# Layer 2 of a four-layer block: one combined weight for attention's way out and the context

## The chip, the cores and the metric

The kernel runs on one NeuronCore of a Trainium2 chip. Five engines work side by side, each through its own list of instructions in order: TensorE (PE in the profile, with its weight loads as PEld), VectorE (DVE), ScalarE (ACT), GpSimd (POOL) and SyncE (SP, which issues most of the DMA). They wait for each other by semaphores. The metric is the device time of one execution in microseconds (us); smaller is better. Two kernels are compared by executions on the same chip.

## What is computed

The program is four layers over x of shape 8 x 512 x 128 (float32). Each layer has a sequence mixer s and a gate g, and adds s times silu(g) to x. The change lies in the mixer of layer 2, which after a layernorm and causal attention with 16 heads does this (cut to what matters):

```python
attn = attn @ out_w + out_b
x = x + attn
ctx = attn.reshape(b * s, d)
xs = _ln(x, g1, b1).reshape(b * s, d)
vs = jnp.zeros_like(xs)
def step(carry, _):
    xs, vs = carry
    u = jnp.tanh(ctx @ w_ctx + xs @ w_x + b_inl)
    vn = vs + DT * (u - xs - vs)
    xn_ = xs + DT * vn
    return ((xn_, vn), None)
(xs, vs), _ = jax.lax.scan(step, (xs, vs), None, length=NUM_ITERS)   # 8
x = x + xs.reshape(b, s, d)
h = _ln(x, g2, b2)
x = x + (gelu(h @ ff_w1 + ff_b1) @ ff_w2 + ff_b2)
```

`attn` is used twice: added to x, and, through `w_ctx`, as a constant term of the eight steps of the recurrence. The gate of layer 2 is a feed-forward net of five products with two gelu layers of width 512 (`ffn` in the kernel).

## The kernel before

**Layout.** A sequence has 512 tokens. Tiles are either token-major (128 tokens on the partitions, 4 tiles of 128 features) or feature-major (128 features on the partitions, 512 tokens along the row). Matmuls give feature-major results from a weight as the stationary operand; a change of layout is four PE transposes (`to_features`, L168) and a copy out of PSUM.

**Units.** `layer2` walks over 128 units: 8 sequences, 4 head groups g, 4 key blocks kc. Per unit PE is given, in this order: the scores of the unit in `weights` (L1462, output `pu<-qT,kT`, which ACT turns into exp at L1498); a first `fill`; the scores for the row maxima of a unit nine ahead in `maxima` (L1462, output `pu<-kT,qT`, with the causal mask added at L1474 and the maximum taken by DVE at L1477 into `mpad`); a second `fill`; and the weighted sums of the unit two behind in `sums` (L1511). Widths go with kc: scores of 512, 384, 256 and 128 columns, and maxima of 512 columns (a 128x1024 reduction for two heads) once in four units. `put_maxima` (L1484, L1488) subtracts the maxima for a pair of groups.

**Fills.** Everything else comes as generators whose steps are put between these. `fill` takes one step of `groups` if there is one, otherwise one step of `rest` (but none in the second fill of an even unit), and then as many steps of `front` as a credit in passes allows. The number that a step yields is its charge.

- `front` is `begin` of the next sequence (layernorm, transposes to `xT2` and, with scale and bias on DVE at L172, `xa2`; projections L1395 and L1398 to `kT2` and `qT2`, L1409 to `va2`), and its `ffn` (L1427/L1428, then L1443 with gelu at L1444, then L1451).
- `groups` is `group`: for each head group, L1525 to `yb2`. After the last group of a sequence it goes on with `yb2` transposed to `yT2` (a step), the product with `out_w` in both layouts (L1539, added to `xn2` on DVE at L1540; and L1542, evacuated by ACT as `ctx2` at L1544; a step), and the product with `w_ctx` (L1547, copied by ACT to `cw2` at L1549; a step).
- `rest` follows when `group` is at its end: the layernorm of `xn2` into `hr2` (one step; L1286, L1288, L1304 on ACT, L1306, L1310, L1296 on POOL, L1290), its transposes L168 (a step), eight iterations (L1565 on PE, L1567 on DVE, tanh L1568 on ACT, L1572 and L1573 on DVE; each a step), the transposes L1578 with L1579 on DVE and the second layernorm into `hr2` (one step), L168 and L172 (a step), L1588 with gelu at L1589 (two steps of two products), and L1596 (two steps).

The steps of sequence b's `group` end and `rest` thus run among the units of sequence b+1. What is left after the last unit, the end of `group` and the `rest` of sequence 7, is handed to layer 3 as `k.tail`, which takes one step of it per unit of its own.

**Order.** On PE the order of the program text is kept (`manual_schedule`). In layer 2 a scheduler sets the order on DVE, ACT and POOL. PSUM banks are given out by tag: two for `pa` (all products above but the scores, sums and L1443), two pairs for `pu`, one each for `pf` and `ph`. A product waits until the last reader of its bank's former content is through.

Of the kernel before, what the change touches and what calls it, by code (L numbers as in the profile page):

```python
# [10 lines left out]
F32 = mybir.dt.float32  # L11
# [3 lines left out]
AF = mybir.ActivationFunctionType  # L15
# [5 lines left out]
P = 128  # L21
B = 8
T = 512
# [12 lines left out]
class Pack:  # L36


    def __init__(self):
        self.parts, self.at, self.n = [], {}, 0  # L40
# [32 lines left out]
def bc(ap, axis, n):  # L73

    a = ap.unsqueeze(axis)
    shape = list(a.shape)
    shape[axis] = n
    return a.to_broadcast(shape)
# [889 lines left out]
class Layer1:  # L968
# [40 lines left out]
    @staticmethod  # L1009
    def by_head(va):  # L1010
        return va[:, :, 0 : H * 9].rearrange("p j (h d) -> p j h d", d=9)
# [302 lines left out]
class Layer2(BySequence):  # L1314


    def __init__(self, k, ctx, late, x, A, at):
        self.k, self.x = k, x
        nc, tc = k.nc, k.tc

        pool = lambda name, bufs=1: ctx.enter_context(
            tc.tile_pool(name="l2" + name, bufs=bufs, reuse_waits="tile", side="left")
        )
        right = lambda name, bufs=1: late.enter_context(
            tc.tile_pool(name="l2" + name, bufs=bufs, reuse_waits="tile", side="right")
        )
        cp = right("c")
        self.cn = cn = k.load_consts(cp, A["c2"], at[0], "c2")
        ap = pool("f")
        self.fn = fn = k.load_consts(ap, A["f2"], at[1], "f2")  # L1330

        self.half_s = ap.tile([P, 4], F32, name="half_s")
        nc.vector.tensor_scalar(self.half_s, fn["w1_s"], 0.5, None, ALU.mult)
        self.both_s = ap.tile([P, 4], F32, name="both_s")
        nc.vector.tensor_tensor(self.both_s, self.half_s, fn["w2_s"], ALU.mult)
        self.out_bc = cp.tile([P, 1], F32, name="out_bc")
        nc.vector.tensor_scalar(self.out_bc, cn["out_bc"], 100.0, None, ALU.mult)


        self.g1 = cp.tile([P, 2], F32, name="g1_2")  # L1340
        nc.vector.tensor_scalar(self.g1[:, 0:1], cn["g1"], 100.0, None, ALU.mult)
        nc.vector.tensor_scalar(self.g1[:, 1:2], cn["b1"], 100.0, None, ALU.mult)

        self.va2 = [ap.tile([P, JT, H * 9 + 23], F32, name=f"va2{i}") for i in range(2)]
        for t in self.va2:
            nc.gpsimd.memset(t, 0.0)
            nc.gpsimd.memset(self.by_head(t)[:, :, :, 8:9], 1.0)

        self.mpad = [ap.tile([P, JT, P], F32, name=f"mpad{i}") for i in range(2)]
        for t in self.mpad:  # L1350
            nc.gpsimd.memset(t, 0.0)
        self.sp2 = right("p", 2)
        self.tp = right("t", 2)
        self.bp = pool("b", 2)
        self.ep = pool("e", LAG + 2)
        self.q = {}

    @staticmethod
    def by_head(va):
        return va[:, :, 0 : H * 9].rearrange("p j (h d) -> p j h d", d=9)  # L1360

    def begin(self, b):

# [155 lines left out]
    def group(self, b, g):  # L1519

        k, nc, cn, tp, q = self.k, self.k.nc, self.cn, self.tp, self.q[b]
        oT = q["oT"]
        ps = k.pa((P, JT, P))
        for qt in range(JT):
            nc.tensor.transpose(ps[:, qt, :], oT[:, qt * P : (qt + 1) * P], k.ident)  # L1525
        v = ps.rearrange("p t (h d) -> p t h d", d=32)
        den = self.sp2.tile([P, JT, 4], F32, name="den2")
        nc.vector.reciprocal(den, v[:, :, :, 8])
        o = q["yb"].rearrange("p t (a i v d) -> p t a i v d", a=2, i=4, v=2)[:, :, g // 2, :, g % 2, :]
        nc.vector.tensor_tensor(o, v[:, :, :, 0:8], bc(den, 3, 8), ALU.mult)  # L1530
        yield 1.25
        if g < 3:
            return
        sT = tp.tile([P, T], F32, name="yT2", bufs=1)
        k.to_features(q["yb"], sT, nt=JT)
        yield 1.25
        ps = k.pa((P, JT, C))
        for j in range(JT):
            nc.tensor.matmul(ps[:, j, :], sT[:, j * P : (j + 1) * P], cn["out_w"], start=True, stop=True)  # L1539
        nc.vector.tensor_tensor(q["xn"], q["xn"], ps, ALU.add)  # L1540
        ps = k.pa()
        nc.tensor.matmul(ps, cn["out_w"], sT, start=True, stop=True)  # L1542
        ctx = tp.tile([P, T], F32, name="ctx2", bufs=1)
        nc.scalar.activation(ctx, ps, AF.Identity, bias=self.out_bc, scale=100.0)  # L1544
        yield 2.25
        ps = k.pa()
        nc.tensor.matmul(ps, cn["w_ctx"], ctx, start=True, stop=True)  # L1547
        q["ctx"] = tp.tile([P, T], F32, name="cw2")
        nc.scalar.copy(q["ctx"], ps)  # L1549
        yield 1.0  # L1550

    def rest(self, b):

# [61 lines left out]
def layer2(k, x, A, at):  # L1615

    late = ExitStack()
    with ExitStack() as ctx:
        ctx.enter_context(k.banks("l2p", pu=2, pf=1, pa=2, ph=1))
        L = Layer2(k, ctx, late, x, A, at)  # L1620
        units = [(b, g, kc) for b in range(B) for g in range(4) for kc in range(JT)]
        held = {}
        ctx.enter_context(k.tc.manual_schedule(engines={mybir.EngineType.PE}))
        for _ in L.begin(0):
            pass
        U = 4 * JT
        PAIR = 2 * JT
        AHEAD = PAIR + 1
        def maxima(u):

            b, g, n = units[u]
            L.maxima(b, g, (n - 1) % JT)

        first = L.ffn(0)
        for u in range(AHEAD):
            maxima(u)
            next(first, None)
        L.put_maxima(0, 0)
        for _ in first:
            pass  # L1640
        front = groups = rest = iter(())
        credit = 0.0

        def fill(u, second):


            nonlocal credit
            wide = 1.5 - u % JT
            share = (2.4 + 0.6 * wide, 2.4 - 0.6 * wide)[second] if u >= U else 1.8
            share += 0.3 - 0.6 * second  # L1650
            passes = next(groups, None)
            if passes is None:
                passes = 0.0 if second and u % 2 == 0 else next(rest, 0.0)
            credit = min(credit, share) + share - passes
            while credit > 0.0:
                passes = next(front, None)
                if passes is None:
                    break
                credit -= passes

        for u in range(len(units) + LAG):
            b, n = divmod(u, U)
            if u < len(units):
                held[u] = L.weights(*units[u])
                if u % PAIR == PAIR - 1 and u + 1 < len(units):
                    L.put_maxima(units[u + 1][0], units[u + 1][1] // 2)
            fill(u, False)
            if u + AHEAD < len(units):
                maxima(u + AHEAD)
            fill(u, True)  # L1670
            if u >= LAG:
                wb, g, kc = units[u - LAG]
                L.sums(wb, g, kc, held.pop(u - LAG))
                if kc == JT - 1:
                    groups = chain(groups, L.group(wb, g))
                    if g == 3:
                        rest = chain(rest, L.rest(wb))

            if n == LAG - 1 and b + 1 < B:
                front = chain(L.begin(b + 1), front, L.ffn(b + 1))  # L1680
        assert next(front, None) is None
        k.tail = chain(groups, rest), late.close
# [634 lines left out]

PACKS = (pack0, pack1, pack2, pack3)
LAYERS = (layer0, layer1, layer2, layer3)


# [35 lines left out]
```

## Time and profile before

The time before is 3589.2 us, the median of three runs (3583.16 to 3598.02). One execution was profiled.

| | us |
|---|---|
| profiled execution, whole | 3592.12 |
| its span, first to last instruction | 3590.4 |
| layer 2's units in it, from 1461 to 2560 | 1099 |
| PE / DVE / ACT / POOL busy, whole span | 2891.0 / 2323.1 / 1793.6 / 733.4 |
| mean granted TensorE clock, whole span | 0.861 |
| ACT table loads at L1498, L1444, L1589 | 66, 55, 14 of 1.283 us |

How to read it: a matmul in float32 appears as two PE rows, so L1547's eight products are "x16". "Idle before" of a group is time in which its engine had nothing running just before an instruction of the group, with the releaser that ended it. PEld is a queue of its own in the profile: a wait there need not hold up PE if a matmul is still running. PEclk is the granted share of TensorE's full clock. In timeline rows the columns are start, duration, engine, line, operation, names and shape, count, and in brackets the idle time before with its releaser. The notation `128x512` is partitions by elements.

### The profile page before, as it was taken

To read this page: it belongs to the slowest core of one execution; us is meant where nothing else is said; L and a number is where in the kernel's file an instruction comes from. 1 tells how busy PE (TensorE), PEld (TensorE's weight loads), DVE (VectorE), ACT (ScalarE), POOL (GpSimd) and SP (SyncE) were. 2 spreads that over 40 slices of the span, in tenths; PEclk is the share of its full clock that TensorE was granted. 3 is DMA by queue.
4 is the path that set the end of the run, shared out by engine and by line. 5 is a ranking of instruction groups with operands and counts; after the bars stand their busy time and mean duration, and the time that the engine had idled before them with its cause. 6 is when DMAs were issued, how large, how long until landed. Compare 5 with 4: busy or idle time off the path is not lost.

```text
span 3590.4 us, 46304 instructions
## 1 busy us (share of the span) xinstructions
PE 2891.0 (81%) x16950; PEld 1591.5 (44%) x16950; DVE 2323.1 (65%) x6354; ACT 1793.6 (50%) x3386; POOL 733.4 (20%) x845
## 2 busy tenths in 40 slices
PE   6175868635998799698888888898789888888887
PEld 4154656534444454334434333443334444454453
DVE  7999888896583334534454554554577767777776
ACT  4173646422444355243545454455466556566655
POOL 0012131300124553211111111111112122222221
PEclk8587889766789999898999999999788888888888
DMA  4012121211001222100000000000000000000000
GB/s 121 2 30 44 32 52 32 43 49 48 1 13 35 40 42 27 45 1 1 1 1 1 1 1 1 1 1 1 21 1 1 4 1 4 4 1 7 4 1 6
DMA packets 67522, 64.59 MB, mean 18 GB/s; under 512 B 5344, under 2 KB 59616, under 8 KB 66784
## 3 DMA queue, kind: packets, MB, share of 16 engines
q1 hardware_dynamic: 39264, 42.75, 3.9%
q0 software_dynamic: 19712, 14.69, 3.1%
q10 hardware_dynamic: 8320, 4.19, 0.4%
q8 instruction: 133, 2.18, 0.2%
q14 instruction: 93, 0.76, 0.1%
HBM read 43.80 MB, written 17.83 MB: 17 GB/s over the span
## 4 chain that ended last, share of the span: by engine, by line
PE 36%; DVE 14%; ACT 10%; issue 2%; POOL 1%; DMA 0%; POOLq 0%; ACTq 0%; DVEq 0%
PE pu L1462 6%; PE ph L1443 5%; PE pu L2102 4%; DVE nm L2104 3%; PE pf L2132 2%; ACT at L2107 2%; PE pf L1511 2%; ACT at L1498 2%; ACT L1498 2%; DVE mpad L1477 1%; PE pa L1565 1%; PE pa L2145 1%; PE pu L1474 1%; PE pa L1596 1%; PE pa L2034 1%
## 5 line engine op out<-in xcount | busy, mean ns | idle before, releaser
L2107 ACT ACTIVATE at<-pu,nm 128x512 f32<-128x512 f32 x512 | 347.7, 690 | 226.8 <-DVE nm L2104 225.3
L2102 PE MATMUL pu<-qT,kT 32*128 32x512 f32 x1024 | 296.3, 740 | 79.3 <-ACT at L2107 79.1
L2104 DVE TENSOR_REDUCE nm<-pu 128x1 f32<-128x512 f32 x512 | 318.7, 680 | 39.6 <-PE pu L2102 39.2
L199 POOL TENSOR_SCALAR_AFFINE_SELECT at<-at 128x512 f32<-128x512 f32 x184 | 124.4, 676 | 1029.2 <-ACT at L1498 879.7
L1477 DVE TENSOR_REDUCE mpad<-pu 128x2 f32<-128x1024 f32 (+3 forms) x256 | 198.9, 818 | 151.1 <-PE pu L1474 151.0
L1128 ACT ACTIVATE at<-pu,rsqrt 128x1024 f32<-128x1024 f32 (+3 forms) x256 | 190.9, 792 | 188.2 <-PE pu L1123 164.1
L1443 PE MATMUL ph<-hid,f 128*128 128x512 f32 x512 | 256.9, 629 | 11.6 <-ACT hid L1444 11.5
L1498 ACT ACTIVATE at<-pu 128x1024 f32<-128x1024 f32 (+3 forms) x256 | 167.1, 701 | 163.6 <-PE pu L1462 162.5
L364 PE MATMUL pa<-HR,ident 128*128 128x128 f32 x512 | 127.4, 417 | 140.3 <-DVE HR L765 140.3
L2102 PEld LDWEIGHTS pu<-qT,kT 32*128 32x128 f32 x1024 | 100.2, 209 | 178.4 <-ACT at L2107 159.4
L364 PEld LDWEIGHTS pa<-HR,ident 128*128 128x128 f32 x512 | 112.4, 265 | 150.1 <-DVE HR L765 74.7
L2132 PE MATMUL pf<-at,va 128*32 128x512 f32 x1024 | 161.3, 708 | 11.9 <-POOL va L2119 11.9
L608 POOL DMA_INDIRECT f_d<-ys,idx x48 | 90.3, 1881 | 382.2 <-ACT ys L607 352.8
L1462 PE MATMUL pu<-kT,qT 32*128 32x512 f32 (+3 forms) x1024 | 136.2, 504 | 30.4 <-ACT at L1498 29.6
L1443 PEld LDWEIGHTS ph<-hid,f 128*128 128x128 f32 x512 | 94.8, 200 | 114.1 <-issue 90.1
L1462 PE MATMUL pu<-qT,kT 32*128 32x512 f32 (+3 forms) x1024 | 128.1, 496 | 20.3 <-DVE mpad L1477 19.9
L1123 PE MATMUL pu<-qT,kT 32*128 32x512 f32 (+3 forms) x1024 | 131.4, 519 | 5.8 <-ACT at L1128 4.9
L2119 POOL TENSOR_TENSOR va<-V,sm 128x32 f32<-128x32 f32 x128 | 34.5, 270 | 488.8 <-DVE sm L2118 428.6
L1066 POOL DMA_INDIRECT f_d<-ys,idx x64 | 103.4, 1616 | 135.1 <-DMA f_d<-ys,idx 86.1
L1498 ACT ACT_TABLE_LOAD x66 | 84.7, 1283 | 90.1 <-PE pu L1462 89.3
L1133 DVE TENSOR_TENSOR at<-at,ceiling 128x512 f32<-128x512 f32 x72 | 49.9, 694 | 106.5 <-ACT at L1128 102.5
L691 ACT COPY Y<-pa 128x128 f32<-128x128 f32 x32 | 8.4, 263 | 208.4 <-PE pa L364 208.4
(621 smaller groups left out, 6806.2 us busy)
## 6 DMA issues: line engine op xcount, KB each, us to landing
w<-in_w_dram SPq DMA_DIRECT2D x24, 512.0 KB
f_d<-zeros ACTq DMA_DIRECT2D x8, 512.0 KB, 5.7
xn_d<-xn SPq DMA_DIRECT2D x8, 512.0 KB, 3.2
w<-in_w_dram SPq DMA_DIRECT2D x16, 256.0 KB, 2.9
w<-in_w_dram SPq DMA_DIRECT2D x24, 128.0 KB, 2.1
f<-in_f_dram SPq DMA_DIRECT2D x1, 2888.0 KB
xn<-in_x_dram SPq DMA_DIRECT2D x4, 512.0 KB, 7.1
Gt<-in_x_dram SPq DMA_DIRECT2D x4, 512.0 KB, 5.0
```

The lines of the kernel that those rows point to most:

```text
L199: self.nc.gpsimd.affine_select(a, a if src is None else src, pattern, ALU.is_ge, 0.0, base=0, channel_multiplier=-1)
L364: nc.tensor.matmul(ps, k.ident, src[:, :, i], start=(i == 0), stop=(i == 7))
L1123: nc.tensor.matmul(pu[:, n, 0:m], q["kT"][r, g // 2, kc * P : kc * P + P], q["qT"][r, g, kc * P :], start=True, stop=True,)
L1128: nc.scalar.activation(at_[:, i : i + 2, 0:m], pu[:, :, 0:m], AF.Square, bias=k.rsqrt2, scale=32.0**-0.5)
L1443: nc.tensor.matmul(ps, fn[n][:, c0 : c0 + P], src[:, i, :], start=(i == 0), stop=(i == 3))
L1462: self.k.nc.tensor.matmul(pu[:, n, 0:m], a[r, c0 : c0 + P], b[r, q0 : q0 + m], start=True, stop=stop)
L1477: nc.vector.tensor_reduce(top[:, i : i + 2, 16 + g % 2], pu[:, :, 0:m], AX.X, ALU.max)
L1498: nc.scalar.activation(at_[:, i : i + 2, 0:m], pu[:, :, 0:m], AF.Exp, scale=8.0**-0.5)
L2102: nc.tensor.matmul(pu, q["kT"][r, kc * P : (kc + 1) * P], q["qT"][r, g, :], start=True, stop=True)
L2104: nc.vector.tensor_reduce(nm[:, n : n + 1], pu, AX.X, ALU.max, negate=True)
L2107: nc.scalar.activation(E[:, n, :], pu, AF.Exp, bias=nm[:, w], accum_out=sm[:, w])
L2132: nc.tensor.matmul(po[i * 32 : i * 32 + 32, :], va[:, kc, c0 : c0 + 32], E[:, i, :], start=(kc == 0), stop=(kc == JT - 1))
```

## The change

The two products in a row, with `out_w` (scaled by 100, plus bias) and with `w_ctx`, are linear. The changed kernel multiplies the two weight matrices once, on the chip, and gives the bias the same treatment; each sequence then multiplies `yT2` by the joint matrix and evacuates it straight to `cw2`. `join` is called once, between `put_maxima(0, 0)` and the remaining steps of the first `ffn`. In `group` the third step of the end (L1547, L1549, `yield 1.0`) is gone, so the generator has a step fewer, and `ctx2` is not needed.

```diff
@@ Layer2.__init__
+        self.both_w = cp.tile([P, P], F32, name="both_w")
+        self.both_b = cp.tile([P, 1], F32, name="both_b")
@@ Layer2
+    def join(self):
+
+        k, nc, cn = self.k, self.k.nc, self.cn
+        turned = self.tp.tile([P, P], F32, name="turned2", bufs=1)
+        ps = k.pa((P, 3, P))
+        nc.tensor.transpose(ps[:, 0, :], cn["out_w"], k.ident)
+        nc.vector.tensor_copy(turned, ps[:, 0, :])
+        nc.tensor.matmul(ps[:, 1, :], turned, cn["w_ctx"], start=True, stop=True)
+        nc.tensor.matmul(ps[:, 2, 0:1], cn["w_ctx"], self.out_bc, start=True, stop=True)
+        nc.vector.tensor_copy(self.both_w, ps[:, 1, :])
+        nc.vector.tensor_copy(self.both_b, ps[:, 2, 0:1])
@@ Layer2.group
         ps = k.pa()
-        nc.tensor.matmul(ps, cn["out_w"], sT, start=True, stop=True)
-        ctx = tp.tile([P, T], F32, name="ctx2", bufs=1)
-        nc.scalar.activation(ctx, ps, AF.Identity, bias=self.out_bc, scale=100.0)
+        nc.tensor.matmul(ps, self.both_w, sT, start=True, stop=True)
+        q["ctx"] = tp.tile([P, T], F32, name="cw2")
+        nc.scalar.activation(q["ctx"], ps, AF.Identity, bias=self.both_b, scale=100.0)
         yield 2.25
-        ps = k.pa()
-        nc.tensor.matmul(ps, cn["w_ctx"], ctx, start=True, stop=True)
-        q["ctx"] = tp.tile([P, T], F32, name="cw2")
-        nc.scalar.copy(q["ctx"], ps)
-        yield 1.0
@@ layer2
         L.put_maxima(0, 0)
+        L.join()
         for _ in first:
             pass
```

In the changed kernel's own line numbers the joint product is L1556 and its evacuation L1558; lines below L1338 shift by 2, then by 14, and below `group` by 9.

## Prediction

> **What bounds the kernel now.** I read the page's slices first, to find the stage of layer 2, then the busy times of that stretch, what TensorE waited for in it, and last the timeline around the edited step. Columns of the first view: stretch, us, busy us (and instructions) of PE, PEld, DVE, ACT, POOL, granted clock, DMA share, GB/s.
> ```profile
> 1461.00:2560.00 1099.00, 969.42 (x5464) 433.24 (x5465) 540.21 (x867) 519.98 (x666) 137.42 (x180) 0.94 0.01 2
> ```
> PE is busy 969 of 1099 us, DVE and ACT about half. Layer 2 is a stream of matmuls in a fixed order with some 130 us of holes; what counts is PE work and the holes. PE's waits in this stretch (us in total, times, longest):
> ```profile
> PE pu L1462 <- ACT at L1498: 29.6, 37, 1.9
> PE pu L1462 <- DVE mpad L1477: 19.9, 18, 3.0
> PE pa L1395 <- DVE xa L172: 12.8, 4, 5.4
> ...
> PE pa L168 <- DVE hr L1290: 5.4, 4, 3.4
> ```
> No wait on what the edited lines write is among the large ones: the removed product is PE work, not a stall. But hr, the layernorm of `rest`, already keeps PE waiting, and the edit moves it.
>
> **Part 1, the product that goes** (busy us, mean ns | idle before):
> ```profile
> L1547 PE MATMUL pa<-ctx,c 128*128 128x512 f32 x16 | 9.6, 685 | 0.8 <-ACT ctx L1544 0.8
> L1549 ACT COPY cw<-pa 128x512 f32<-128x512 f32 x8 | 4.7, 586 | 3.1 <-PE pa L1547 2.5
> ```
> Eight products leave 9.6 us of PE and 4.7 us of ACT, about 1.2 and 0.6 us a sequence; L1542 and L1544 stay, with other operands. The ACT copy lies under PE work and I count it at nothing; if it were on the path it would be worth 4.7. The matmul's worth depends on what follows it, part 3.
>
> **Part 2, `join`.** PE: a 128x128 transpose, a 128x128 product and a one-column product, between L1484 and the next L1443. On DVE its first copy stands behind the two L1488 operations (1.41 us from 1497.28). PE reached the next L1443 at 1497.08. With join the transpose runs beside L1488; the copy, by the nearest DVE row of 128x128 (L1530, 0.29 us), is done at 1499.0; the products, at the 0.275 us a row of L1539, end at about 1499.5. So **+2.4 us** once, in a stretch where PE runs back to back. Ends: 1.4 (PE's wait covers part of the gelu wait of 0.78 us behind it) and 4 (another operation gets ahead on DVE). The wait holds up L1443 alone; its L1444 on ACT has nothing else to do there.
>
> **Part 3, one step fewer in `group`.** This moves everything in `rest` one fill earlier, and there the sum is decided. In the instruction order of the two built programs, `rest`'s layernorm, iterations and hidden products keep their number but slip from one fill of a unit to the other.
>
> *First layernorm and projections.* On DVE the chain xn, s, hr, ss, hr goes ahead of the 128x1024 maxima, and these ahead of xa and qT. Sequence 3's projections in before, during the `rest` of sequence 1:
> ```profile
> 1801.19 0.69 DVE L1290 TENSOR_TENSOR hr<-hr,rs 128x512 f32<-128x512 f32 x1 [1.20 <-POOL rs L1296]
> 1801.80 2.35 DVE L1477 TENSOR_REDUCE mpad<-pu 128x2 f32<-128x1024 f32 x2
> 1804.07 0.80 DVE L172 TENSOR_SCALAR xa<-pa,c 128x512 f32<-128x512 f32 x1
> 1805.02 2.05 PE L1395 MATMUL pa<-xa,c 128*128 128x512 f32 x2 [5.44 <-DVE xa L172]
> ```
> PE stands 5.44 us for xa. From the end of L1539 (1795.97) this chain takes 5.9 us to hr, 7.1 to the first maximum (which frees the bank of the next scores L1462), 9.05 to xa. In the new order, by `rest` of sequence: 1 and 3: the h transposes are one fill earlier, xa is written before the chain, both pairs of projections run inside the old hole, and the second L1398 then waits for qT at 9.1; that ends at 10.2, one cool microsecond more, L1511 and the scores 2: all is done 13.0 us after L1539. In before, the same set ends at 17.5 (1813.43) and 17.1 (2076.70): -4.5 and -4.1. 5: one pair fits into the hole: 14.0 against 17.4, -3.4. 0: L1409 (1.1 us) fits: -1.1. 2 and 6: the hole before L1462, ended by the maximum at 7.1 us, just grows by the product removed: 0. 4: now this one gets the xa wait: +0.5. Sum **-12.6**; this holds the removed matmuls of seven sequences. Ends -6 (the qT wait cools PE further) and -18.
>
> *Second layernorm.* In before:
> ```profile
> 1738.69 0.40 PE L1474 MATMUL pu<-neg_b,ident_b 128*128 128x128 bf16 x4
> 1739.55 2.35 DVE L1477 TENSOR_REDUCE mpad<-pu 128x2 f32<-128x1024 f32 x2
> 1744.09 0.66 PE L1578 MATMUL pa<-ident,X 128*128 128x128 f32 x4 [0.43 <-DVE X L1573]
> 1744.78 0.69 DVE L1579 SCALAR_TENSOR_TENSOR xn<-pa,xn 128x512 f32<-128x512 f32 x1 [0.75 <-PE pa L1578]
> 1750.31 0.69 DVE L1290 TENSOR_TENSOR hr<-hr,rs 128x512 f32<-128x512 f32 x1 [1.14 <-POOL rs L1296]
> 1751.08 0.65 PE L168 MATMUL pa<-ident,hr 128*128 128x128 f32 x4
> ```
> From L1578's end (1744.75) to hr (1751.00) are 6.25 us, and PE has just that much queued between: two L1443 pairs, L1462 twice, L1511. In the new order L1578 stands in the second fill, right after the 128x512 maxima matmuls, and L168 in the next one: between them only one L1443 pair, L1511 and L1462. Also DVE has both 128x1024 maxima before L1579. With L1578 at 1738.95: maxima until 1741.45; L1579 and its followers (0.7+0.7+0.6+0.3+0.7), the square on ACT 0.65, ss 0.9, the power on POOL 1.05, hr 0.7: hr at 1747.8. PE is through with L1462 at 1743.2. A **stall of 4.6 us**, behind which all of PE's work queues; POOL and SP lose nothing by it.
>
> What it costs net: in before, PE's idle time from 1738.96 to 1769.26 is 30.30-27.11 = 3.2 us (by the windows), in waits for X, hid, at and qT. Going through the new order with the same rows, these shrink to 0.3, since ACT and DVE catch up in the stall and the two L1588 pairs run in neighbouring fills: 4.6+0.3-3.2 = +1.7.
>
> To that comes the clock. The Trainium skill, "TensorE: Matmul & The Clock Gate", section "Why this matters for your kernels", wants no PE gap over about 3 us: a whole idle window sends the clock back to half, and by its Part 1 that lasts for some 3.4 us of work. This rule speaks against the change. The trace agrees and is harsher: after 5.44 us the granted clock was 0.50 from 1804.0 to 1810.8, with L1395 at 2.05 us where it takes 1.02; after 2.72 us two more pairs took 2.08 and 1.92 (2199.36). By the rule one window, 3.4 us at half speed, costs 1.7 us; by the row, 6.8 us, 3.4. A 4.6 us gap doesn't always cover a whole window, so I take 2.2. Together about **+4** per sequence, for sequences 0 to 5: +24. Ends: 1.5 (nothing cooled, more absorbed) and 7. In sequence 6 no maxima are left and L168 waits 3.44 us already: +1.
>
> *Table loads.* In layer 2 the changed order has 128 instead of 135, in layer 3 one fewer, as the four gelus of L1589 stand together. The skill, "ScalarE: Activation LUTs", section "What ACT_TABLE_LOAD costs", gives a switch 1283 ns plus 1380 ns of draining. Here
> ```profile
> 1751.23 1.28 ACT L1498 ACT_TABLE_LOAD   x1 [2.97 <-PE pu L1462]
> 1752.52 1.51 ACT L1498 ACTIVATE at<-pu 128x768 f32<-128x768 f32 x2
> 1754.05 1.28 ACT L1444 ACT_TABLE_LOAD   x1
> ```
> the load follows the last exp within 0.02 us and the exp the load: no drain is seen. By the rule seven loads are 18.6 us, by the row 9.0, on an engine half idle. Those at L1589 are in the +1.7 already; for the rest -1 (ends 0 and -8).
>
> *Tail.* Sequence 7's `group` and `rest` run in layer 3. L168 waits 3.94 us for hr at 2565.05 just behind L1547: the removed cover becomes wait, 0. The shorter tail releases `parameters(0)` a unit sooner; layer 3's other due units don't move: 0, ends -3 and +4.
>
> **Sum:** 2.4-12.6+24+1-1 = +13.8 us on the profiled execution's 3592.1 (span 3590.4 and 1.7 around it), so 3605.9. This execution was 0.08% over the median of 3589.2; scaled, **3603 us, slower by 0.4%**, just inside the 0.5% (18 us) that a measurement can tell from no change.
>
> **Rivals.**
> *Faster, 3579:* the 4.6 us stall is a breather. For it: 111 us of waits on exp stand before L1462 when weight loads are counted (29.6 PE, 81.9 PEld), and they could give up as much. Then sequences 0 to 5 cost nothing, and 2.4-12.6+1-1 = -10.2, or -17 and more if the other loads leave the path and the first part nears its end: 3565 to 3585. It decides from a net cost per stall under 1.7 us, 10.2/6. Against it: at this place the trace has just 3.2 us of idle time to give.
> *Clearly slower, 3625:* every stall cools PE for 6.8 us: 6 x 7 = 42, and the qT wait leaves -8 of the first part: 2.4-8+42 = +36. For it speak the six gaps of 2.7 us or more that I looked at, all followed by matmuls at half speed; against it, that idle gaps of 1 us behind ACT are now often cooled too and would go.
> *Nothing to see, 3589:* PE reaches L1578 later too, as X is late on DVE; then hr is less late for L168, the holes just change place, and gain and loss balance.
> That the product isn't saved is excluded: the new order has eight matmuls and eight copies fewer.
>
> **Numbers.** Forecast (3595 to 3616) 0.45; clearly slower 0.26; faster 0.20; balanced 0.09. Of the forecast, 0.20 lies over 3607; of faster, 0.13 below 3571. So faster 0.13, same 0.41, slower 0.46. Range: from the middle of faster to the clearly slower, 3578 to 3628.
>
> **What would show it.** PE's wait at L168 for hr rises from 5.4 us to over 20 in layer 2, six of them near 4 us, each in front of L1443, L1427 or L1451. The wait for xa falls to one of about 6 us. L1556 follows L1539 at 1.0 us a pair. PE busy in layer 2 falls by about 8 us at equal clock, its mean clock from 0.94 to 0.93. Wrong it would be if L1579 stood before the maxima in time, or if `at` waits fell by as much as hr waits rise.

## The result and the profile after

| | before | after |
|---|---|---|
| median, us (4 runs each) | 3588.7 | 3628.1 |
| lowest to highest | 3583.2 to 3598.0 | 3621.5 to 3629.5 |
| profiled execution / its span | 3592.1 / 3590.4 | 3621.5 / 3619.8 |

The ratio is 1.0101, with a 95% interval of 1.0082 to 1.0121: the changed kernel is slower by 1.0%. The forecast was 0.4%, just under the 0.5% that it took for the least that can be told from no change. The direction was right; the size was that of the rival of 3625 us, at the upper end of the range and outside the 3595 to 3616 of the forecast itself.

Layer 2 from the first projection to the first scores of layer 3, in before and then in after (the columns are those of the prediction's first view, whose stretch ended a little sooner):
```profile
1461.00:2577.60 1116.60, 979.45 (x5490) 438.01 (x5490) 547.25 (x878) 525.45 (x675) 138.43 (x181) 0.93 0.01 2
```
```profile
1463.00:2608.50 1145.50, 979.14 (x5483) 440.36 (x5484) 552.96 (x884) 511.54 (x661) 139.36 (x181) 0.93 0.01 2
```
So PE is as busy as it was though eight products are gone, and 28.9 us were added: its idle time grew by 29.2, what half speed costs (half of the time that PE was busy at half clock) by 3.9, and its work at full speed fell by 4.2. That is nearly all of the 29.4 us between the profiled executions; before layer 2 there are 2.0 more, in layer 3 1.5 less.

PE's waits in layer 2 after (us in total, times, longest):
```profile
PE pa L168 <- DVE hr L1290: 37.9, 8, 6.1
PE pu L1476 <- ACT at L1512: 26.9, 37, 1.9
...
PE ph L1457 <- ACT hid L1458: 20.1, 16, 3.1
PE pu L1476 <- DVE mpad L1491: 14.9, 15, 3.0
PE pa L1574 <- DVE X L1582: 10.6, 12, 2.9
PE pa L1409 <- DVE xa L172: 10.2, 4, 6.3
```
The wait for hr, the last of before's waits that the prediction showed, is now the first: 34.5 of its 37.9 us lie in layer 2 (the other 3.4 in layer 3's first microseconds), against 5.4. The gelu wait (L1457 for hid) is 20.1 us; over the same stretch of before it was
```profile
PE ph L1443 <- ACT hid L1444: 11.5, 12, 1.8
```
Exp, maxima and xa together fell by 12.

The edited place itself, the same `rest` (of sequence 0) that the prediction's timeline showed of before:
```profile
1740.68 0.40 PE L1488 MATMUL pu<-neg_b,ident_b 128*128 128x128 bf16 x4
1740.95 0.66 PE L1587 MATMUL pa<-ident,X 128*128 128x128 f32 x4
1741.00 2.36 DVE L1491 TENSOR_REDUCE mpad<-pu 128x2 f32<-128x1024 f32 x2
1743.27 0.68 DVE L1588 SCALAR_TENSOR_TENSOR xn<-pa,xn 128x512 f32<-128x512 f32 x1
1744.04 1.14 PE L1476 MATMUL pu<-qT,kT 32*128 32x512 f32 x8
1748.81 0.64 POOL L199 TENSOR_SCALAR_AFFINE_SELECT at<-at 128x512 f32<-128x512 f32 x1
1748.88 1.11 DVE L1290 TENSOR_TENSOR hr<-hr,rs 128x512 f32<-128x512 f32 x1 [1.14 <-POOL rs L1296]
1750.05 1.12 PE L168 MATMUL pa<-ident,hr 128*128 128x128 f32 x4 [4.87 <-DVE hr L1290]
1750.96 3.62 PE L1457 MATMUL ph<-hid,f 128*128 128x512 f32 x4
1755.41 1.94 PE L1457 MATMUL ph<-hid,f 128*128 128x512 f32 x4
```
The transposes L1587 stand right behind the mask products; on DVE both 128x1024 maxima go ahead of L1588; PE has done its scores (L1476) at 1745.2 and stands 4.87 us. What follows is cold, at half clock (granted 0.50 from 1749 to 1755): the same four rows of L1457 take 3.62 us at 1750.96 and 1.94 at 1755.41. Over `rest` of sequences 0 to 5 this wait is 4.9, 6.1, 6.1, 4.9, 4.1 and 4.9 us, in 6 it is 3.5 (before: at most 1.0, and 3.4).

The other part of the forecast, sequence 3's projections, now beside the first layernorm of sequence 1's `rest`:
```profile
1807.20 1.02 PE L1556 MATMUL pa<-yT,both_w 128*128 128x512 f32 x2
...
1809.46 1.08 PE L1409 MATMUL pa<-xa,c 128*128 128x512 f32 x2
1810.38 1.02 PE L1412 MATMUL pa<-xa,c 128*128 128x512 f32 x2
1811.32 1.13 PE L1409 MATMUL pa<-xa,c 128*128 128x512 f32 x2
1813.22 1.12 PE L1412 MATMUL pa<-xa,c 128*128 128x512 f32 x2 [0.78 <-ACT kT L1410]
```
The wait of 5.44 us for xa is gone and nothing is at half clock (granted 1.00 from 1803 to 1818): from the end of L1553 (1807.4) to the end of the scores that follow (1816.7) are 9.4 us, where before took 17.5 and the forecast had 13.0.

To see the rest, I cut layer 2 into its units and averaged their lengths over the six sequences after the first (my own arithmetic from the traces, us per sequence; a `rest` of sequences 0 to 5 lies in each):

| units of a sequence | what of `rest` runs there | before | after | forecast of the step |
|---|---|---|---|---|
| 0 to 1 | the last products | 14.4 | 17.0 (+2.6) | 0 |
| 2 to 4 | joint product, first layernorm | 28.6 | 26.2 (-2.4) | -2.1 |
| 5 to 11 | iterations | 58.4 | 56.8 (-1.6) | 0 |
| 12 to 15 | second layernorm, L1597 | 30.6 | 36.9 (+6.3) | +4 |
| sum | | 131.9 | 136.9 (+4.9) | +1.9 |

Units 0 and 1 were in no step of the prediction. There (sequence 2 of the units) the trace after shows
```profile
1778.37 2.00 PE L1605 MATMUL pa<-c,hid 128*128 128x128 f32 x16
...
1782.16 1.98 PE L1457 MATMUL ph<-hid,f 128*128 128x512 f32 x4
...
1783.22 1.92 ACT L1512 ACTIVATE at<-pu 128x1024 f32<-128x1024 f32 x2
1785.16 1.28 ACT L1458 ACT_TABLE_LOAD   x1
1786.46 0.69 ACT L1458 ACTIVATE hid<-ph,f 128x512 f32<-128x512 f32 x1
1787.20 1.98 PE L1457 MATMUL ph<-hid,f 128*128 128x512 f32 x4 [3.05 <-ACT hid L1458]
```
and before
```profile
1775.00 2.05 PE L1596 MATMUL pa<-c,hid 128*128 128x128 f32 x16
...
1777.80 0.49 PE L1462 MATMUL pu<-kT,qT 32*128 32x128 f32 x4 [0.75 <-ACT at L1498]
...
1779.37 1.94 PE L1443 MATMUL ph<-hid,f 128*128 128x512 f32 x4
```
In before the last product of `rest` takes the first fill, and `front` gets one step of L1443 behind the maxima (L1462 with `kT,qT`), in the second. In after `rest` is over one fill earlier, the first fill belongs to `front` alone, and it puts two such steps into it. The second needs the bank that the gelu of the first reads, and that gelu stands on ACT behind a pair of exps and a table load: 3.05 us of PE idle. The +2.6 is a mean of unequal parts: in the six sequences these two units changed by -0.9, +4.0, +1.9, -0.2, +8.2 and +2.5 us. Waits of about 3 us for gelu stand in the second and the fifth alone, and of the fifth's +8.2, 4.6 are half clock.

### The profile page after: what moved, and what is told of

Read it like the earlier page. It is cut to its first block, busy times and chain, and to the rows that moved or that the text cites. A ratio compares the mean times of both kernels' runs of the same rounds, so it can differ in the third digit from the quotient of the medians.

```text
span 3619.8 us, 46267 instructions
## 1 busy us (share of the span) xinstructions
PE 2897.7 (80%) x16939; PEld 1597.7 (44%) x16939; DVE 2326.4 (64%) x6357; ACT 1777.8 (49%) x3370; POOL 733.1 (20%) x845
## 4 chain that ended last, share of the span: by engine, by line
PE 36%; DVE 14%; ACT 10%; issue 3%; POOL 2%; DMA 1%; POOLq 0%; ACTq 0%; DVEq 0%
PE ph L1457 5%; PE pu L1476 5%; PE pu L2112 5%; DVE nm L2114 3%; PE pf L2142 3%; ACT at L1512 2%; DVE mpad L1491 2%; ACT at L2117 2%; PE pf L1525 2%; ACT L1512 1%; PE pa L2155 1%; PE pa L1574 1%; PE pu L1488 1%; ACT u L1577 1%; PE pu L1123 1%
## 5 line engine op out<-in xcount | busy, mean ns | idle before, releaser
L199 POOL TENSOR_SCALAR_AFFINE_SELECT at<-at 128x512 f32<-128x512 f32 x184 | 123.1, 669 | 980.3 <-ACT at L1512 830.9
L1457 PE MATMUL ph<-hid,f 128*128 128x512 f32 x512 | 264.7, 646 | 20.3 <-ACT hid L1458 20.1
L2142 PE MATMUL pf<-at,va 128*32 128x512 f32 x1024 | 166.9, 731 | 12.8 <-POOL va L2129 12.8
L1476 PE MATMUL pu<-kT,qT 32*128 32x512 f32 (+3 forms) x1024 | 134.8, 499 | 27.6 <-ACT at L1512 26.9
L1457 PEld LDWEIGHTS ph<-hid,f 128*128 128x128 f32 x512 | 96.8, 204 | 128.9 <-issue 97.0
L1476 PE MATMUL pu<-qT,kT 32*128 32x512 f32 (+3 forms) x1024 | 128.2, 501 | 15.2 <-DVE mpad L1491 14.9
L1476 PEld LDWEIGHTS pu<-kT,qT 32*128 32x128 f32 x1024 | 57.4, 190 | 124.9 <-ACT at L1512 75.6
```

Source lines behind the costliest of these rows:

```text
L199: self.nc.gpsimd.affine_select(a, a if src is None else src, pattern, ALU.is_ge, 0.0, base=0, channel_multiplier=-1)
L1457: nc.tensor.matmul(ps, fn[n][:, c0 : c0 + P], src[:, i, :], start=(i == 0), stop=(i == 3))
L1476: self.k.nc.tensor.matmul(pu[:, n, 0:m], a[r, c0 : c0 + P], b[r, q0 : q0 + m], start=True, stop=stop)
L2142: nc.tensor.matmul(po[i * 32 : i * 32 + 32, :], va[:, kc, c0 : c0 + 32], E[:, i, :], start=(kc == 0), stop=(kc == JT - 1))
```

## The experiments

Theory A, the place: the loss comes from `rest` standing one fill earlier, by the wait for hr at the second layernorm and the half clock behind it. Its rivals: the joint product or `join` themselves make it (theory B); `front`, which no longer pays the 1.0 of the removed step, runs ahead and bunches its steps (theory C); or the wait only takes the place of idle time that was there anyway. All ratios are to the kernel before, run on the same chip.

**1. Put the lost step back.** The changed kernel with an empty step where the removed one was:
```diff
@@ group, after the joint product
         yield 2.25
+        yield 1.0
```


> The changed kernel with one empty step put back at the end of group, with the old charge of 1.0: TensorE's order is then that of the kernel before, only without the second product and with join. Theory A (the loss comes from rest moving one fill earlier): the time falls back to the kernel before. Since in that order the hole behind L1539 ends with the DVE maximum or xa, not with TensorE's work, the removed product gives nothing and join costs 2.4 us: 3588 to 3593. Theory B (the joint product and join themselves cost): it stays near 3625. A plain count of the removed work would give 3581.

Measured: 3588.2 against 3583.2 us, ratio 1.0014 (1.0007 to 1.0021). With the step back the loss is gone, as theory A had it, and with it the gain: a kernel with eight products and eight copies fewer isn't faster than before. In its layer 2
```profile
1449.10:2564.00 1114.90, 970.66 (x5483) 435.62 (x5483) 548.16 (x881) 520.80 (x667) 138.42 (x181) 0.93 0.01 2
```
PE's idle time is 144 us against 137 in before. Where the product stood PE now waits longer, for the maxima and for xa (19.9 and 12.8 us in the prediction's list):
```profile
PE pu L1476 <- DVE mpad L1491: 25.1, 19, 3.9
PE pa L1409 <- DVE xa L172: 14.6, 4, 6.3
```

**2. Take only the step away.** The kernel before, both products as they were, in one step:
```diff
@@ group, after the product with w_ctx
-        yield 1.0
```


> The kernel before with the last yield of group deleted and nothing else: both products stay, rest moves one fill earlier. Theory A: as slow as the changed kernel or a little slower by the kept product, 3624 to 3636, with TensorE waiting 4 to 6 us for hr before the second L168 of six sequences. Theory B: like the kernel before, 3589.

Measured: 3611.2 us, 1.0073 (1.0050 to 1.0096). No joint product, no `join`, nothing saved, and most of the loss is there. PE's waits in it:
```profile
PE pa L168 <- DVE hr L1290: 37.6, 8, 6.1
...
PE ph L1443 <- ACT hid L1444: 20.3, 16, 3.1
```
are those of the changed kernel within 0.3 us, and the waits for hr in sequences 0 to 5 are the same six, to 0.01 us. Its layer 2 takes 1147.7 us, all of the loss there (1145.5 in the changed kernel). With run 1 this settles that the missing step is the cause, and not the products: putting it back removes the loss, taking it alone makes it. The step is both a place and a charge of 1.0, and these two runs move both; run 3 parts them. The time is below the 3624 to 3636 expected; why the ratio is smaller, on another chip, I don't know.

**3. The step at no charge.** As run 1, but the empty step costs `front` no credit:
```diff
@@ group, after the joint product
         yield 2.25
+        yield 0.0
```


> The changed kernel with one empty step put back that charges nothing: rest has its old place, but front keeps the share of 1.0 that the change gave it. Theory A (place of rest alone): like the run with the charged step, 3586 to 3597. Theory C (front running ahead and bunching its steps, seen as longer waits of L1457 for gelu, is a good part of the loss): 3602 to 3615.

Measured: 3548.1 against 3583.2 us, 0.9899 (0.9874 to 0.9925). This was in neither theory's range: it beats both kernels. Charged alike, the changed kernel and this one differ in the place of the steps alone, and that is worth 2% (1.0101 to 0.9899; 0.9918 in the repeat below). At the same place, runs 1 and 3 differ in the charge alone, worth 1.2% the other way. So the 1.0% of the change is what is left of a larger loss by the place and a gain by the charge. Runs 8 to 10 take it up.

**4. An empty step at the second layernorm.** The changed kernel with the layernorm and its transposes L168 one fill further apart:
```diff
@@ rest, after L1588 and the second layernorm
         yield 1.25
+        yield 0.0
```


> The changed kernel with one empty, uncharged step between the second layernorm and its transposes: the first layernorm and the projections keep their new place, the second transposes get a fill more. Theory A, with the 4 to 6 us waits for hr as the main cost: these waits go, about 32 us of idle time and up to 10 us of half clock come back: 3588 to 3602. Theory C: only a part, 3608 to 3620, since the bunched front steps stay.

Measured: 3562.0 us, 0.9946 (0.9924 to 0.9967), better than expected. PE doesn't wait for hr at all in sequences 0 to 5 and 0.4 us in 6. Units 12 to 15 fall from 36.9 to 32.8 us. Units 0 and 1 fall too, from 17.0 to 14.7, since the empty step also puts the end of `rest` a fill later. So this run takes away both losses, and keeps the shorter units 2 to 11.

**5. and 6. No second layernorm.** Both kernels without it: the transposes take xn instead of hr, so the normalisation is left out, and PE has nothing to wait for.
```diff
@@ rest
-        self.layernorm(xn, h)
...
-        k.to_features(h, hT, nt=JT, scale=cn["g2"], bias=cn["b2"])
+        k.to_features(xn, hT, nt=JT, scale=cn["g2"], bias=cn["b2"])
```
Of the changed kernel:

> The changed kernel without the second layernorm of layer 2's mixer (its input goes unnormalised into the transposes; the output is another one). If the waits for hr before the second L168 are the main loss (idle and half clock, 5.9 us per sequence at that unit), they go and 30 to 45 us come back: ratio to the kernel before 0.997 to 1.003. If the loss lies in the bunched front steps and the other moved steps, the ratio stays over 1.005.

Of the kernel before, as the control:

> The kernel before without the same second layernorm: its waits for hr are only 5.4 us in layer 2, so the ratio should be 0.996 to 1.000. It is the control for the run above: if leaving the layernorm out gains as much here, the gain there says nothing of the wait.

Measured: 3570.1 us, 0.9946 (0.9926 to 0.9967), and 3577.0 us, 0.9975 (0.9966 to 0.9984), against 3586.7. Without the chain the changed kernel falls from 1.0101 to 0.9946, by 1.55% and a little further than expected, and the other by 0.25%, as expected: the main loss sits behind the second layernorm, and what the layernorm takes in itself is small. Units 0 and 1 still take 17.4 us: the gelu wait there has another cause.

**7. Fill the wait with useless work.** The changed kernel with four products of 128x128 by 128x512 per sequence, whose result nobody reads, between the second layernorm and its transposes:
```diff
@@ rest, after the second layernorm
         yield 1.25
+        ps = k.pa()
+        for _ in range(4):
+            nc.tensor.matmul(ps, cn["w_x"], last, start=True, stop=True)
```


> The changed kernel with four useless 128x128x512 products in front of the second transposes, where TensorE otherwise stands still for hr; some 4.1 us of work per sequence. If the half clock after the wait is caused by the idle time, the clock stays up: about 1.9 us per sequence come back, 8 to 14 us in all, ratio 1.006 to 1.008, although work was added. If the clock falls for other reasons, no gain: 1.010 to 1.013.

Measured: 3614.1 us, 1.0074 (1.0050 to 1.0097). The same place:
```profile
1737.97 3.70 PE L1593 MATMUL pa<-X,c 128*128 128x512 f32 x8
1743.00 0.63 PE L168 MATMUL pa<-ident,hr 128*128 128x128 f32 x4 [1.33 <-DVE hr L1290]
1743.46 1.88 PE L1457 MATMUL ph<-hid,f 128*128 128x512 f32 x4
```
hr comes no sooner, but PE works 3.70 us of the time, and L1457 behind it takes 1.88 us instead of 3.62. In layer 2 the useless products are 27 us of work, 23 us of idle time went, and half speed costs 17 us less (my sums over the traces): 12.8 us shorter than the changed kernel, though hr came no sooner. In units 12 to 15 the cost of half speed falls from 2.8 us a sequence to 0.8. So the half clock behind these waits has a price of its own. In the times it is 0.27%, as expected, but the two intervals overlap by a little.

**8. The kernel before with a free step.** Is run 3's gain the joint product or only the credit?
```diff
@@ group, after the product with w_ctx
-        yield 1.0
+        yield 0.0
```


> The kernel before with the charge of group's last step lowered from 1.0 to 0.0 and nothing else. If the 1.2% between the two kernels with an empty step put back is due to front's larger share alone, it shows here too, without any joint product: ratio 0.987 to 0.993. If it needs the removed product, 0.997 to 1.000.

Measured: 3573.7 against 3586.7 us, 0.9960 (0.9943 to 0.9978), less than run 3 gave, but on another chip. So both once more, side by side:

> The changed kernel with the lost step back in its place at a charge of 0.0, once more, on the same chip and in the same rounds as the kernel before with that charge. If the saved product counts once PE has other work to put into the hole: 0.988 to 0.992 of the time before, and at least 0.3% faster than the kernel before with a free step. If all of the gain is the charge: the two are equal within 0.3%.

> The kernel before, with the charge of the last step of group set from 1.0 to 0.0 and nothing else. If the saved product counts only with free work beside it: 0.994 to 0.997 again, behind the changed kernel with a free step by 0.3% or more. If all of the gain is the charge: equal to it within 0.3%.

Measured against 3595.7 us: 3567.3, 0.9918 (0.9901 to 0.9935), and 3574.5, 0.9947 (0.9928 to 0.9966). The intervals overlap, and the two profiled executions have spans of 3567.5 and 3567.8 us. Their stretches of layer 2, the changed kernel of run 3 first, then the kernel before with a free step in its second profile:
```profile
1449.30:2535.30 1086.00, 951.23 (x5479) 427.15 (x5479) 547.46 (x881) 518.73 (x665) 139.14 (x181) 0.96 0.01 2
```
```profile
1461.10:2544.00 1082.90, 953.23 (x5490) 427.80 (x5490) 546.31 (x878) 523.25 (x673) 139.47 (x181) 0.96 0.01 3
```
Against run 1's row, both are 29 and 32 us shorter, PE is busy 19 and 17 us less, and the clock is 0.96 instead of 0.93. One changed number does this without the joint product. Whether the product adds anything to it stays open: of the repeat's executions on one chip the joint product's is the faster in 33 of 36 pairs, by 0.2% in the medians, but the two profiles show nothing of it in layer 2 (1092 us with the product joined, 1083 without).

**9. and 10. More of the same.** Run 3 with the joint product's charge lowered too, and run 3 with run 4's empty step:
```diff
@@ group, after the joint product (9)
-        yield 2.25
+        yield 1.25
+        yield 0.0
```
```diff
@@ group, after the joint product (10)
         yield 2.25
+        yield 0.0
@@ rest, after the second layernorm (10)
         yield 1.25
+        yield 0.0
```


> The changed kernel with the free step, and the charge of the joint product lowered too, from 2.25 to 1.25, so that front gets a further pass in its fill. If more work of front in the fills of group's end is always good: 0.980 to 0.987. If one pass was what the hole there took and more of it only bunches gelu steps: 0.990 to 1.000.

> The changed kernel with the free step at group's end and an empty step between the second layernorm and its transposes. If the wait for hr still costs something with the free step: 0.982 to 0.988. If with rest back in its old fills the wait is gone and the step only pushes L1588 to later fills: 0.989 to 1.000.

Measured: 3577.6 us, 0.9950 (0.9934 to 0.9967), and 3577.7 us, 0.9953 (0.9936 to 0.9971). Either is worse than run 3 in the same rounds. In run 9 PE waits more for xa (16.5 us) and for gelu (16.4). Run 10's layer 2 is about as short as run 3's (1088 against 1086 and, in the repeat, 1092 us), and layer 3 behind it takes 10 us longer than in the repeat, 5 longer than in run 3.

The units of some of these, in us per sequence as in the table above, with what half speed cost over the six sequences (before 43, after 47):

| | 0 to 1 | 2 to 4 | 5 to 11 | 12 to 15 | sum | half speed |
|---|---|---|---|---|---|---|
| step put back (1) | 14.1 | 28.2 | 58.8 | 30.6 | 131.7 | 39 |
| step taken away (2) | 17.5 | 26.1 | 56.7 | 36.7 | 137.2 | 47 |
| step at no charge (3) | 14.7 | 26.1 | 55.8 | 31.0 | 127.6 | 18 |
| the same, repeat | 14.7 | 26.5 | 55.5 | 31.4 | 128.2 | 24 |
| before, no charge (8, first) | 15.0 | 26.0 | 55.9 | 31.7 | 128.6 | 25 |
| before, no charge (8, second) | 14.7 | 25.6 | 55.9 | 31.0 | 127.1 | 14 |
| second layernorm apart (4) | 14.7 | 25.5 | 57.1 | 32.8 | 129.8 | 27 |

The free step has the good half of both kernels: units 0, 1 and 12 to 15 as before, 2 to 11 as after. The short units 2 to 11 go with the freed charge and not with the place of `rest`: in all kernels of this and the former table that have it, units 2 to 4 take 25.5 to 26.5 us and 5 to 11 take 55.5 to 57.1, with `rest` in either place; with the charge of 1.0 they take 28.2 to 28.6 and 58.4 to 58.8. Of the 25 us between runs 1 and 3 in this table, 21 are half speed, and of the 21 us to the repeat, 15; two profiles of one kernel differ in this by 6 to 11 us. In layer 2 gaps of PE over 2.5 us number 9 in before, 15 in after, 10 in run 1, 6 in run 3 and 4 in run 8. Which of the gaps the extra credit closes, and why a further pass (run 9) opens others, I haven't followed through.

## Why the prediction was half right

**The product's worth** (Part 1): right that what follows decides. Its removal with the order kept was worth nothing, and neither was the copy on ACT that went with it (run 1). Where the prediction let the removed matmuls count, in the first part's -12.6, the product gave no gain: run 2, which keeps it, has units 2 to 4 at 26.1 us like the changed kernel.

**`join`** (Part 2): +2.4 forecast; from the start of L1498 behind `join`'s place to the next L1457 the trace has 2.77 us, where before had 0.44: +2.3.

**First layernorm and projections** (Part 3): -12.6 over six sequences forecast, -2.4 times 6, -14, measured. The two waits of 5.4 us for xa in the `rest` of sequences 1 and 3 went and one of 6.3 us came in that of sequence 4, as worked out; the second projection's wait, priced with a cold clock, was 0.78 us without one. The reason is in part another one: the prediction put the gain to the step that is gone, and by runs 1 and 3 it goes with that step's charge, which the prediction does not mention.

**Second layernorm** (Part 3): the mechanism was right to the instruction: the same order on PE and DVE, a stall forecast at 4.6 us and measured at 4.1 to 6.1, a clock loss forecast at 2.2 and measured at 2.0 (half-speed loss of units 12 to 15, 0.8 before, 2.8 after). That is nearer to its 1.7 for one window than to the 3.4 that it read off the row; there it halved 6.8 us of half clock, of which PE was busy for 5.8. **The step that failed is the term "net +1.7"**: the prediction let the other idle time around L1578 shrink from 3.2 us to 0.3, because ACT and DVE would catch up in the stall. Measured, the idle time of these units rose from 2.9 to 7.1 us: 5.2 in the unit with L168, and 2.0 in the three behind it where before had 2.1. The stalls were 5.2 us in the mean, so some 1 us was absorbed and not 2.9. So a sequence lost 6.3 us and not 4, which makes +14 over six. One part of that has a cause of its own: hr took 1.11 us, not 0.69 (last section).

**Missed altogether:** the units at the end of `rest`, +2.6 us a sequence in the mean, +16, where two gelu products now come in one fill. I followed the moved steps to where `rest` begins and where it waits, and not to where it ends and leaves its fill to `front`. Against it stand the iterations' units, 1.6 us a sequence shorter, -10, also not forecast; they too go with the freed charge, and which of their waits gave way I didn't follow. That these two misses have opposite signs is luck.

**Table loads and tail**: the whole execution had 242 loads of ACT's tables against 250, as forecast, and no time of its own is to be seen in that. Layer 3 was 1.5 us shorter, with 0 forecast and -3 to +4 as the ends.

**The sum:** the six sequences were forecast at +1.9 each and took +4.9, 18 us more; with 2.3 for `join` and about -3 at the end this gives the 28.9 us by which layer 2 grew. **The rivals:** the breather is refuted by runs 5 and 6, since without the wait the changed kernel gains 1.3% more than the kernel before. The slower rival came near in its sum, +36, but not by its mechanism: the clock behind the stalls cost 2.0 us and not 3.4, and the rest was idle time that didn't close and the units at the end of `rest`.

## What to carry to other kernels

In a stream of steps that is shared out by turns and credits, a removed step moves everything behind it: follow its queue to the end, and ask who gets the turn that comes free and what two of its steps in a row wait for. A latency chain that another engine's queue can get ahead of needs its cover counted in instructions on each engine; an empty step between the chain's start and its reader restored that here, and the end of `rest` with it (1.0101 to 0.9946). Don't credit a stall with idle time that it "absorbs" unless the same engine is seen to catch up, and when a step goes, ask separately what its place and what its charge did. Try the charges of such a plan as sizes in their own right: one such number in the kernel before was worth 0.4 to 0.5%.

## What the runs showed of the hardware

A product that does nothing can shorten a stage: filling 3.7 us of a wait kept the granted clock at 1.00 behind it instead of 0.50, and the matmuls there ran in 1.88 instead of 3.62 us (run 7). Stretches at half clock in layer 2 had lengths of mostly 3.4 or 6.8 us, as many in before as in after (26), but 8 of 6.8 us in before and 13 in after. A multiplication on DVE, L1290 of 128x512, written to hr, took 1.11 us in every one of the eight cases of the two kernels in which POOL's L199 ran beside it for 0.57 us. It took 0.69 in 23 others, and 1.75 in one beside 1.20 us of an addition on POOL (L1583). Seven of the eight are second layernorms of the changed kernel, where the new place puts it just behind the exps that L199 follows.
